# Staging table rows in the attention's buffers, and 13 gather buffers instead of 10

## The chip, the core and the metric

The kernel runs on one core of a Trainium2 chip. A core has five engines, each with an instruction queue of its own: TensorE (PE in the profile; PEld is its weight load), VectorE (DVE), ScalarE (ACT), GpSimd (POOL) and SyncE (SP), which only issues transfers here. Sixteen DMA engines move data between HBM, the large memory, and SBUF, the memory on the core; matmuls write to PSUM, which DVE and ACT read. Engines wait for one another by semaphores. The metric is the time of one execution in microseconds (us), from the device.

## The reference

Two layers act on a tensor `x` of 8 images, 256 channels and 64 x 64 points; all is in float32. Each is a group norm (32 groups of 8 channels), a layer, and a residual. The first layer is an attention over each point's 3 x 3 neighbours in 4 heads, to which weights that a small projection generates are added. The second is a deformable convolution: for each output point and each of 9 taps it reads the image at a computed, fractional position.

```python
x = x + _L0_conv_ref(_gn(x), w_qkv, w_kg, b_kg, alpha, beta, w_proj)
x = x + _L1_conv_ref(_gn(x), w_off, b_off, w)
...
# layer 0
qkv = einsum('oc,bchw->bohw', w_qkv, x)
q, k_, v = split(qkv, 3, axis=1)
logits = einsum('bhdl,bhdkl->bhkl', q, patches3x3(k_))
attn_out = einsum('bhkl,bhdkl->bhdl', softmax(logits, axis=2), patches3x3(v))
kernel = einsum('hkc,bhcl->bhkl', w_kg, qkv_by_head) + b_kg
conv_out = einsum('bhkl,bhdkl->bhdl', kernel, patches3x3(v))
out = einsum('oc,bchw->bohw', w_proj, alpha * conv_out + beta * attn_out)
...
# layer 1
om = conv3x3(x, w_off) + b_off                  # 27 channels
off, mask = om[:, :18], sigmoid(om[:, 18:27])   # (dy, dx) of 9 taps; a mask of each
py, px = base_y + ky + off_y, base_x + kx + off_x
y0, x0 = floor(py), floor(px); ly, lx = py - y0, px - x0
v = (samp(y0, x0) * (1 - ly) * (1 - lx) + samp(y0, x0 + 1) * (1 - ly) * lx
     + samp(y0 + 1, x0) * ly * (1 - lx) + samp(y0 + 1, x0 + 1) * ly * lx) * mask
out = einsum('bckhw,ock->bohw', v, w)
```

`samp(y, x)` takes all channels of one point, and zeros outside the image.

## The kernel before, in words

**Two halves run beside each other.** For each image there is a *front*: the attention (`attention`, line 595) and then the preparation of the convolution (`prepare`, line 678). And there is the deformable convolution itself, in the main loop (line 977). While image `b` is convolved, the front of image `b + 1` is issued in small steps between the pieces of the convolution. The generator `fronts` yields after each step. `STEPS` = 144 steps belong to the stretch of one image, about one for each half slot of the main loop (lines 998 to 1002). The front of the first image runs alone at the start, and during the last image there is none.

The order of instructions on PE, ACT, DVE and POOL is the order in which the program calls them (`manual_schedule`, line 949); each engine executes its queue in order. SyncE issues its transfers in order too.

**Table and gathers.** An image is cut into 8 chunks of 8 rows (512 points). In `prepare`, each chunk passes `to_table` (line 684), then `offsets` (18 matmuls, line 710), and one step later `positions` (line 722). `to_table` writes the normalized chunk, transposed to one row per point, to a table in HBM. An entry holds a point's 256 channels and those of the point one image row below; since two entries follow one another, one row of 4 KB fetches all four corners. In three parts per chunk, PE transposes 176 points into PSUM (`ptab`, line 690), ACT copies them to an SBUF tile `ts` (line 696), and SyncE issues two writes of 176 KB from it (line 699), one for each half of the entries. Two tables take turns between images. `positions` turns the offsets into an index and four corner weights for each point and tap.

The convolution of an image is 72 slots (8 chunks x 9 taps) of 4 blocks of 128 points, so 288 blocks. For a block, POOL issues a gather (`gather`, line 838) that fetches one 4 KB row for each of 128 points into a buffer `g`; ACT scales the first corner into a tile `s` (`scale`, line 854); DVE adds the other three in three instructions (`sum_corners`, line 862), after which `g` is free; PE transposes `s` into PSUM (`pt`, line 892); ACT copies that to `vt` (line 895); and four matmuls of a slot's 512 points add to the output `po` (line 917). At the end of a chunk ACT copies `po` to `y` (line 932), DVE adds the residual, and SyncE stores the result (line 939); `r`, the residual, is loaded again from a copy in HBM at line 904.

**How far ahead.** When the main loop stands at block `i`, ACT scales blocks `i` + 8 and `i` + 9 (`SCALE_AHEAD`), DVE sums `i` + 6 and `i` + 7 (`SUM_AHEAD`), and POOL issues the gathers of `i` + `LEAD` and the next, where `LEAD` = `SCALE_AHEAD` + `GATHERS` = 18. There are `GATHERS` = 10 buffers `g` of 4 KB per partition (pool `gp`, line 104). In the last image, `gathers` also has POOL write a mark (`tick`) every fourth block, which DVE copies one slot later (line 872). After some long pieces of the attention POOL copies one element of their result (`held`, line 881), which holds its next gathers until DVE or ACT is done.

**Buffers.** A tag with `bufs=n` names `n` buffers that are used in turn. A tile that takes a buffer over waits until all that read the tile before it, transfers included, are done. The buffers that matter here, per partition: `ts`, six of 2 KB (line 695); `qk`, one of 6.25 KB, with the attention's products of queries and keys (line 373; `logits` reads it); `wk`, four of 2 KB, with the spread attention weights (line 523; `weighted` reads it). An attention's last use of `qk` and `wk` lies before `prepare` begins.

**Other loads.** While the table is written, SyncE also loads the next image in chunks of 512 KB (`load_chunk`, line 93), each after its place in `image` has been normalized for the table. DVE takes their statistics (`first_stats`, line 289), and after the last one `Norm` forms mean and variance (`mv`, line 185); the first matmul of the next attention (`gn`, line 190) needs them.

Of the kernel before, what the change touches and what calls it, by code (L numbers as in the profile page):

```python
# [9 lines left out]
F32 = mybir.dt.float32  # L10
# [8 lines left out]
C = 256  # L19
# [9 lines left out]
HEADS = 4  # L29
# [5 lines left out]
TJ = 6  # L35
TP = R * WP // TJ
# [11 lines left out]
BLOCKS = SLOTS * NB  # L48
SUM_AHEAD = 6
SCALE_AHEAD = SUM_AHEAD + 2  # L50
GATHERS = 10
LEAD = SCALE_AHEAD + GATHERS
STEPS = 2 * SLOTS
STEPS_AHEAD = 12
# [5 lines left out]
def preact_kernel(ctx: ExitStack, tc: tile.TileContext, a: dict, out: bass.AP):  # L60
# [30 lines left out]
    def load_chunk(b, c, queue=nc.sync):  # L91
        s = slice(c * N, (c + 1) * N)
        queue.dma_start(image[:, :, s], sources[b][:, :, s])
# [8 lines left out]
    for c in (0, 2, 4, 6, 7):  # L102
        load_chunk(0, c)
    gp = ctx.enter_context(tc.tile_pool(name="gp", bufs=GATHERS))
    w_qkv = [gp.tile([96, 4, C], F32, tag="g", name=f"w_qkv{i}") for i in range(2)]
# [61 lines left out]
    p1 = ctx.enter_context(tc.tile_pool(name="p1", bufs=1))  # L167
    p2 = ctx.enter_context(tc.tile_pool(name="p2", bufs=2))
# [6 lines left out]
    def psum_a(name):  # L175
        return ps_a.tile([P, 512], F32, tag="a", name=name)
# [501 lines left out]
    def prepare(b, gn):  # L678
# [5 lines left out]
        def to_table(c, xn):  # L684
            for i in range(TJ // 2):
                ps = psum_a(f"ptab_{b}_{c}_{i}").rearrange("p (j e) -> p j e", j=2)
                for j in range(2):
                    o = WP + (2 * i + j) * TP
                    for ct in range(NT):
                        nc.tensor.transpose(  # L690
                            ps[:TP, j, ct * P : (ct + 1) * P],
                            xn[:, ct].rearrange("p r w -> p (r w)")[:, o : o + TP],
                            ident,
                        )
                ts = p2.tile([TP, 2, C], F32, tag="ts", name=f"ts_{b}_{c}_{i}", bufs=6)
                nc.scalar.copy(ts, ps[:TP])
                for q in range(2):
                    e = (R * c + 1 - q) * WP + 2 * i * TP
                    nc.sync.dma_start(
                        table[e : e + 2 * TP, q, :].rearrange("(j p) e -> p j e", p=TP), ts  # L700
                    )
# [92 lines left out]
        for c in range(NC):  # L794
            if om is not None:
                positions(c - 1, om)
            to_table(c, xn)
            yield
            om = offsets(c, xn)
            if b + 1 < B and c > 0:  # L800
                first_stats(b + 1, c - 1)
            if c + 1 < NC:
                xn = normed(xt, gn, c + 1, carry=True)
            if b + 1 < B:
                if c == 0:
                    load_chunk(b + 1, 0)
                if c + 1 < NC:
                    load_chunk(b + 1, c + 1)
            yield
# [22 lines left out]
    def gather(i):  # L832
        if i >= B * BLOCKS:
            return
        b, n = divmod(i, BLOCKS)
        c, k, j = n // NB // KK, n // NB % KK, n % NB
        g = gp.tile([P, 4 * C], F32, tag="g", name=f"g_{i}")
        nc.gpsimd.indirect_dma_start(  # L838
            out=g,
            out_offset=None,  # L840
            in_=tables[b % 2],
            in_offset=bass.IndirectOffsetOnAxis(ap=found[b, c][0][:, j, k : k + 1], axis=1),
        )
        rows[i] = g
# [12 lines left out]
    def sum_corners(i):  # L857

        work = [sums[n] for n in (i, i + 1) if n in sums]
        for q in range(1, 4):  # L860
            for s, g, w in work:
                nc.vector.scalar_tensor_tensor(  # L862
                    s, g[:, q * C : (q + 1) * C], w[:, q : q + 1], s, ALU.mult, ALU.add
                )
# [84 lines left out]
    with tc.manual_schedule(engines=ordered):  # L949
# [8 lines left out]
        for n in range(STEPS_FIRST - 4):  # L958
            next(steps, None)
        for i in range(GATHERS):  # L960
            gather(i)
        for i in range(0, SUM_AHEAD, 2):
# [5 lines left out]
            sum_corners(i)  # L968
            gather(i + GATHERS)
            gather(i + GATHERS + 1)  # L970
            for n in range(2 if i == 0 else 1):
                next(steps, None)
        done = STEPS + STEPS_FIRST
        gather(SUM_AHEAD + GATHERS)
        gather(SUM_AHEAD + GATHERS + 1)
# [105 lines left out]
```

## Time and profile before

| | |
|---|---|
| median of 4 runs | 4811.95 us (4808.81 to 4822.01) |
| profiled execution | 4811.06 us, span 4809.3 us |
| mean granted TensorE clock | 0.988 |
| start, until the first block is transposed | 338 us |
| images 1 to 7, each | 566 to 581 us |
| last image | 443 us |
| DVE line 862, sums | 6912 of 475 ns |
| POOL line 838, gathers | 2304 of 1264 ns |
| PE line 917, convolution | 4608 of 601 ns |
| ACT line 696, copies to `ts` | 192 of 588 ns or less |

The span runs from the first instruction to the last. "PE pt L892 <- DVE s L862" in a view of waits reads: PE stood idle before the instruction of line 892 that writes `pt`, and what released it was DVE's instruction that writes `s`. In a timeline, a row gives start, duration, engine, line, operation, names (out<-in) and a count of merged instructions; the bracket holds the idle time before it and what ended it. In a view of windows, a row gives a stretch, its length, each engine's busy time with its count of instructions, the granted clock, the mean busy share of the DMA engines and their GB/s.

### The profile page before, as it was taken

The numbers are of one execution on the slowest core, as the hardware profiler recorded it, in microseconds if no ns is written. First come the engines' busy times: TensorE is split into PE (matmuls) and PEld (weight loads), VectorE is DVE, ScalarE is ACT, GpSimd is POOL, SyncE is SP. The second block draws the span as 40 slices with busy tenths as digits, with TensorE's granted clock in tenths as the row PEclk, the third lists the DMA queues.
The fourth block names the chain that finished last, engine by engine and source line by source line (L and its number), as shares of the span: only waits on it lengthen the run. The fifth ranks groups of instructions, "written<-read, shape, count | busy, mean of one in ns | idle before, by whom it ended". The sixth has DMA issues, their size and how long they took to land. (4 is left out here: it accounts for less than half of the span.)

```text
span 4809.3 us, 77468 instructions
## 1 busy us (share of the span) xinstructions
PE 4555.1 (95%) x25344; PEld 2362.5 (49%) x25344; DVE 4178.0 (87%) x10177; ACT 2442.1 (51%) x5200; POOL 3005.4 (62%) x2607
## 2 busy tenths in 40 slices
PE   8989999999999999999999999999999899997878
PEld 4444554455544555445544555545554455543434
DVE  5669889899988998899998999889998899987887
ACT  2335555455555555555554555555555455554554
POOL 0027666676656666477675766757666676667786
PEclk9999999999999999999999999999999999999999
DMA  2068789888898888988889888888888888888998
GB/s 98 23 219 289 275 295 335 296 315 297 299 338 302 306 287 286 361 291 306 298 300 346 298 301 286 326 324 285 305 304 326 289 304 288 291 317 333 358 354 311
DMA packets 472353, 1414.03 MB, mean 294 GB/s; under 512 B 46526, under 2 KB 114366, under 8 KB 471820
## 3 DMA queue, kind: packets, MB, share of 16 engines
q0 software_dynamic: 331776, 1208.11, 70.1%
q1 hardware_dynamic: 138156, 197.62, 11.6%
q8 instruction: 199, 3.26, 0.3%
q10 hardware_dynamic: 2016, 3.36, 0.2%
q14 instruction: 206, 1.69, 0.1%
HBM read 1275.97 MB, written 132.94 MB: 293 GB/s over the span
## 5 line engine op out<-in xcount | busy, mean ns | idle before, releaser
L838 POOL DMA_INDIRECT g<-table,idx x2304 | 2911.6, 1264 | 1779.6 <-DVE s L862 622.6
L862 DVE SCALAR_TENSOR_TENSOR s<-g,wt,s 128x256 f32<-128x256 f32 x6912 | 2809.1, 475 | 110.3 <-ACT s L854 98.3
L917 PE MATMUL po<-vt,w_conv 128*128 128x512 f32 x4608 | 2191.2, 601 | 2.1 <-ACT y L932 2.1
L854 ACT ACTIVATE s<-g,wt 128x256 f32<-128x256 f32 x2304 | 1077.6, 509 | 377.0 <-DMA g<-table,idx 297.0
L917 PEld LDWEIGHTS po<-vt,w_conv 128*128 128x128 f32 x4608 | 819.6, 192 | 830.0 <-issue 817.7
L895 ACT COPY vt<-pt 128x512 f32<-128x512 f32 x1152 | 617.2, 588 | 608.2 <-PE pt L892 607.8
L892 PE MATMUL pt<-ident,s 128*128 128x128 f32 x4608 | 654.4, 279 | 121.0 <-DVE s L862 108.5
L892 PEld LDWEIGHTS pt<-ident,s 128*128 128x128 f32 x4608 | 520.7, 141 | 355.9 <-DVE s L862 146.4
L391 DVE TENSOR_TENSOR qk<-qk,near_k 128x400 f32<-128x400 f32 x256 | 134.8, 568 | 238.5 <-PE qk L383 238.5
L710 PE MATMUL om<-xn,w_off 128*32 128x512 f32 x2304 | 288.8, 598 | 0.0
L309 PE MATMUL psq<-xn,w_qkvT 128*128 128x512 f32 x512 | 254.3, 641 | 26.4 <-DVE wk L524 22.9
L340 PE MATMUL psv<-xn,w_qkvT 128*128 128x512 f32 (+1 forms) x576 | 249.8, 560 | 2.1 <-DVE kb L442 2.1
L340 PE MATMUL psk<-xn,w_qkvT 128*128 128x512 f32 (+1 forms) x576 | 246.3, 557 | 0.0
L570 PE MATMUL proj<-acc,w_projT 128*128 128x512 f32 x512 | 239.6, 593 | 1.6 <-ACT acc L564 1.6
L317 ACT COPY q<-psq 128x512 f32<-128x512 f32 x128 | 75.1, 586 | 248.9 <-PE psq L309 248.9
L309 PEld LDWEIGHTS psq<-xn,w_qkvT 128*128 128x128 f32 x512 | 97.5, 200 | 179.3 <-issue 89.3
L351 ACT COPY k<-psk 128x512 f32<-128x512 f32 (+1 forms) x144 | 79.2, 551 | 192.2 <-PE psk L340 192.2
L557 PEld LDWEIGHTS av<-wk,vk 100*64 100x64 f32 x4096 | 130.9, 138 | 92.3 <-issue 34.1
L710 PEld LDWEIGHTS om<-xn,w_off 128*32 128x32 f32 x2304 | 74.3, 109 | 200.5 <-issue 161.7
L544 ACT COPY vk<-vk 100x512 f32<-100x512 f32 x256 | 137.4, 587 | 69.7 <-PE vk L539 69.4
L340 PEld LDWEIGHTS psk<-xn,w_qkvT 128*128 128x128 f32 x576 | 104.1, 190 | 123.1 <-issue 118.7
L340 PEld LDWEIGHTS psv<-xn,w_qkvT 128*128 128x128 f32 x576 | 103.3, 190 | 118.0 <-issue 114.6
(102 smaller groups left out, 3439.9 us busy)
## 6 DMA issues: line engine op xcount, KB each, us to landing
table<-ts SPq DMA_DIRECT2D x384, 176.0 KB
g<-table,idx POOLq DMA_INDIRECT x2304
x<-in_x_dram SPq DMA_DIRECT2D x61, 512.0 KB
x<-x SPq DMA_DIRECT2D x56, 512.0 KB
r<-x SPq DMA_DIRECT2D x56, 512.0 KB
out_dram<-r SPq DMA_DIRECT2D x56, 512.0 KB
out_dram<-y SPq DMA_DIRECT2D x7, 512.0 KB
w_conv<-in_w_conv_dram SPq DMA_DIRECT2D x1, 2304.0 KB
```

The costliest lines, as they stand in the source:

```text
L309: nc.tensor.matmul(ps, w_qkvT[:, ct, m * P : (m + 1) * P], window(self.xn, ct, 4), start=(ct == 0), stop=(ct == NT - 1),)
L340: nc.tensor.matmul(ps[:, : (hi - lo) * W], w_qkvT[:, ct, o : o + P], self.xn[:, ct, lo:hi, 1 : W + 1], start=(ct == 0), stop=(ct == NT - 1),)
L391: nc.vector.tensor_mul(qk[:, 2 * jj : 2 * jj + 2, :, h, :], both[h][:, : 4 * NK].rearrange("p (j c k) -> p j c k", j=2, c=NT), near_k.unsq ...
L544: nc.scalar.copy(self.vk[:, 2 * j : 2 * j + 2, :].rearrange("p t c -> p (t c)"), ps[:NK])
L570: nc.tensor.matmul(ps, w_projT[:, ct, m * P : (m + 1) * P], self.acc[:, ct].rearrange("p (t y x) -> p y t x", y=T, x=T), start=(ct == 0), ...
L710: nc.tensor.matmul(ps[32 * g : 32 * g + 32, :], w_off[:, ct, k, :], window(xn, ct, k), start=(n < 4), stop=(n >= KK * NT - 4),)
L838: nc.gpsimd.indirect_dma_start(out=g, out_offset=None, in_=tables[b % 2], in_offset=bass.IndirectOffsetOnAxis(ap=found[b, c][0][:, j, k : ...
L854: nc.scalar.activation(s, g[:, 0:C], AF.Copy, scale=w[:, 0:1])
L862: nc.vector.scalar_tensor_tensor(s, g[:, q * C : (q + 1) * C], w[:, q : q + 1], s, ALU.mult, ALU.add)
L892: nc.tensor.transpose(pt[ct][:, j, :], s[:, ct * P : (ct + 1) * P], ident)
L895: nc.scalar.copy(v[:, ct, :], pt[ct].rearrange("p b n -> p (b n)"))
L917: nc.tensor.matmul(po[m], w_conv[:, ct, k, m * P : (m + 1) * P], v[:, ct, :], start=(k == 0 and ct == 0), stop=(b + 1 < B and k == KK - 1 ...
```

## The change

Three more gather buffers are kept, 13 for 10, so `LEAD` becomes 21. The room comes from `ts`, whose six buffers of 2 KB go. For an odd chunk, the three parts are tiles of the tag `wk`, one of its four buffers after another. For an even chunk, one tile of the tag `qk` holds all three parts; ACT copies to a third of it at a time.

```diff
-GATHERS = 10
+GATHERS = 13
 LEAD = SCALE_AHEAD + GATHERS
...
-                ts = p2.tile([TP, 2, C], F32, tag="ts", name=f"ts_{b}_{c}_{i}", bufs=6)
+                if c % 2:
+                    ts = p2.tile([TP, 2, C], F32, tag="wk", name=f"ts_{b}_{c}_{i}", bufs=HEADS)
+                else:
+                    if i == 0:
+                        whole = p1.tile(
+                            [TP, TJ // 2, 2, C], F32, tag="qk", name=f"ts_{b}_{c}"
+                        )
+                    ts = whole[:, i]
                 nc.scalar.copy(ts, ps[:TP])
                 for q in range(2):
                     e = (R * c + 1 - q) * WP + 2 * i * TP
```

## The prediction

> **What bounds the kernel now.** I read the page's engine row first, then the waits of TensorE (PE) over the whole span, then windows, then the timelines of the places where PE waits.
>
> ```profile
> PE 4555.1 (95%) x25344; PEld 2362.5 (49%) x25344; DVE 4178.0 (87%) x10177; ACT 2442.1 (51%) x5200; POOL 3005.4 (62%) x2607
> q0 software_dynamic: 331776, 1208.11, 70.1%
> q1 hardware_dynamic: 138156, 197.62, 11.6%
> ```
> PE is the bound for most of the time, so a change of buffers can only win what PE waits: 4809.3 - 4555.1 = 254 us, and of that only what late gathers cause. The gathers (q0) hold the DMA engines for 70% of the span and SyncE's transfers (q1: table rows, images, outputs) for 12%.
>
> ```profile
> PE pt L892 <- DVE s L862: 108.5, 89, 6.8
> PE gn L190 <- DVE mv L185: 45.1, 9, 9.1
> PE pt L892 <- ACT vt L895: 11.9, 15, 2.6
> ACT s L854 <- DMA g<-table,idx: 297.0, 305, 7.3
> ACT ts L696 <- DMA table<-ts: 31.7, 17, 3.3
> ```
> The first row sounds like the target. By time, though, 80.0 us of it lie in the last image and 11.0 in the seventh. "Image n" here is the time in which the nth image is convolved; from the end of the seventh no next image's work runs beside it. Each of images 1 to 6 has 2 to 5 us. ACT (ScalarE) waits 297 us for gathers, but it is busy for 51%, and most of that reaches nobody.
>
> The windows show where gathers are late: the light stretch at the end of an attention (lines 658 to 676), where little front work slows the convolution.
>
> ```profile
> 1338.00:1376.00 38.00, 32.58 (x149) 16.06 (x148) 30.86 (x80) 18.46 (x36) 29.34 (x27) 1.00 0.97 368
> 1376.00:1456.00 80.00, 75.92 (x471) 35.52 (x469) 73.26 (x213) 39.20 (x87) 31.18 (x32) 1.00 0.98 363
> 1913.00:1951.00 38.00, 33.28 (x145) 16.51 (x144) 30.15 (x77) 18.95 (x37) 29.17 (x25) 0.96 0.98 365
> ```
> The columns are PE, weight loads, DVE (VectorE), ACT and POOL (GpSimd) busy, granted clock, DMA share and GB/s. PE is idle for about 5 of 38 us. From there until the next image's attention begins (second row: the stage that writes the table) DMA is at 0.98. How it starts, on DVE and POOL:
>
> ```profile
> 1325.30 11.95 DVE L862 SCALAR_TENSOR_TENSOR s<-g,wt,s 128x256 f32<-128x256 f32 x30
> 1328.09 9.97 POOL L838 DMA_INDIRECT g<-table,idx  x1 [2.58 <-DVE s L862]
> 1338.37 0.93 POOL L838 DMA_INDIRECT g<-table,idx  x1 [0.30 <-issue]
> 1343.64 0.51 ACT L854 ACTIVATE s<-g,wt 128x256 f32<-128x256 f32 x1 [1.86 <-DMA g<-table,idx]
> 1349.32 0.33 PE L892 MATMUL pt<-ident,s 128*128 128x128 f32 x1 [2.60 <-ACT vt L895]
> 1357.11 0.84 PE L892 MATMUL pt<-ident,s 128*128 128x128 f32 x4 [1.03 <-DVE s L862]
> ```
> DVE runs 30 sums back to back; for that time POOL hangs in one gather (9.97 us instead of 0.93). The ten buffers are used up, ACT waits for the next gather, its copies of `vt` come late behind that wait, and PE stops.
>
> **The change, part by part.** *Removed, added.* No instruction: 192 copies of 588 ns on ACT and 384 table writes on SyncE stay; only their buffers differ. Cost 0 for both.
>
> *The copies' waits.* Before, six `ts` buffers: each copy waits for the copy two chunks earlier to have landed. After, an even chunk fills one buffer of three parts in the place of `qk`, so its first copy waits for all six writes of the chunk two before; an odd chunk rotates through four `wk` buffers, so its first copy waits for nothing recent and the other two for one copy further back. With the landings of the trace's completion records (image 2: chunk 0 done at 1385.2, chunk 2 at 1411.1, chunk 4 at 1430.0; the copies begin at 1385.7, 1410.1, 1430.8), even chunks wait about 1 us more at chunk 4 and odd ones 2 to 3 us less at chunk 3: over all images about 23 us for today's 31.7. Neither counts: ACT waits 2.77 and 1.30 us in chunk 3 of image 2 and PE has no gap over 0.53 us in that stage until its end. The cover is the 18 offset matmuls (10.8 us a chunk) queued on PE. If it is gone, ACT's wait goes through `s` to DVE, which is 92% busy there; that price is in the slower rival.
>
> *`qk` and `wk` at both ends.* The first chunk's copy needs the last attention chunk's readers, done tens of us before; the next image's first `qk` write comes 30 us after chunk 6 has landed (1450.6 in image 2), its first `wk` write later still. Cost 0.
>
> *The first gather of the next image* is issued three gathers earlier, and needs the whole table. Table landed and the issue it now takes: 889.1 and 892.6, 1463.6 and 1467.9, 2038.8 and 2044.7, 2619.2 and 2619.5, 3190.3 and 3195.2, 3766.0 and 3773.9. At most 3 us of POOL waiting with 21 blocks in hand: cost 0. Every gather moves up by three in POOL's queue; the tick and hold copies stay where they are.
>
> *Three more gathers landed when POOL hangs.* POOL issues one per 0.94 + 0.30 = 1.24 us when free, so they are worth 3.7 us of lateness at each light stretch. PE's gaps there (over 0.25 us, on `pt`) are 2.1, 4.2, 2.6, 2.8, 2.6, 2.3 and 2.6 us: 19.2. A gap of 0.6 at the end of each stands without a late gather, so 7 x 0.6 = 4.2 stay: 15.0 go. The stretches of images 3 to 6 also show a clock of 0.96 (third window for image 3), 4 x 0.04 x 38 = 6.0 us. Gain 21.0: 2.0 in image 7, 19.0 in the first six (3.2 each).
>
> *What is late next.* After the stage, PE waits for `gn`: mean and variance need the last chunk of the next image.
>
> ```profile
> 1432.07 8.35 SPq L699 DMA_DIRECT2D table<-ts  x6
> 1440.51 1.82 SPq L939 DMA_DIRECT2D out_dram<-r  x1
> 1442.42 0.62 SPq L93 DMA_DIRECT2D x<-in_x_dram  x1
> 1454.40 1.29 DVE L289 BATCH_NORM_STATS2 stats<-x 128x6 f32<-128x512 f32 x2 [0.50 <-DMA x<-in_x_dram]
> 1456.24 0.38 PE L190 MATMUL gn<-mv,gmat 128*128 128x2 f32 x2 [3.71 <-DVE mv L185]
> ```
> That load stands in SyncE's queue behind the table writes. The six gaps are 5.3, 3.7, 6.4, 3.1, 5.6, 9.1 us, and DVE's wait for the load before them 2.1, 0.5, 3.2, 0, 2.4, 6.3: the gap is 3.1 plus that wait. So a microsecond won earlier is kept only if this load also lands earlier. The granted clock after the gaps (0.66 over 10 us after 5.3, 0.83 after 3.7, 0.61 over 13 us after 9.1) costs 18.7 us for 33.2 us of gap: 0.56 us more per us.
>
> The writes start with PE and so 3.2 us earlier, but refilling 13 buffers takes longer. POOL issues 27 gathers in the 38 us before the stage (0.71 per us, its few small copies counted in) and 32 in its 80 (0.40), so three more take 3 / 0.31 = 9.7 us. During the refill SyncE's six writes take 11.0 and 11.7 us, 0.53 per us, against a need of about 8 transfers per 10.4 us chunk (six writes, an image load, a store or reload: 0.77): 2.3 transfers, or 3.0 us, fall behind. In image 2 SyncE's lag behind the copies drains (8.3 us at chunk 3, 1.3 at chunk 6); in images 3 and 6 it does not (3.6, 5.3 at chunk 6). Ends: 0 and 3.0. I take 1.3, a little under the middle, as four of six drain. The gap grows by 1.3 x 1.56 = 2.0 us in six images: 12.0 back.
>
> The Trainium skill ("DMA: Bandwidth & Descriptors", Queues, rings and completion order) states that each DMA engine takes turns between the queues that have work, whatever their length. By it the table writes keep their share however deep the gathers queue; the trace agrees that they get through, at 0.53 per us. The rule alone would not lengthen a single write, and the sum would be 12.0 us better.
>
> *The last image.* POOL and DVE pace each other there by the tick copies (DVE waits 73.8 us for POOL's marks); the gather issued at block `i` reuses the buffer of block `i` + LEAD - GATHERS = `i` + 8, before and after, so the pace of 1.5 us a gather stays. What changes is the stock at its start. Upper end 3 x 1.5 = 4.5 us. Lower end 0: DVE's run of 30 sums at 4332.75 would go on over the three landed blocks, and POOL, hanging from 4335.55 for 9.98 us, would hang longer by as much. I take the middle, 2.2.
>
> The Trainium skill ("SBUF — State Buffer", SBUF: two separate sides) speaks against the change here: DVE can hold a port pair that GpSimd needs for its descriptors, and the loser blocks for whole instructions. By it a deeper stock only lengthens the block, and this term would be 0.
>
> *Sum.* 19.0 + 2.0 - 12.0 + 2.2 = 11.2 us. The profiled execution took 4811.06 us (span 4809.3), the median of the runs is 4811.95; less 11.2 that is 4799.9 to 4800.8, and I say **4800**.
>
> **The rivals.** *Hidden anyway*: DVE's longer runs lengthen POOL's hangs in every light stretch, or the load for `gn` gives all back. For it: the gap at `gn` follows that load. Against it: at 1337.25 DVE's run ends at the projection, not for want of blocks. Image 7's 2.0 stays: 4809.
>
> *All kept*: the lag drains in every image, 19.0 + 2.0 + 4.5 = 25.5: 4786. For it: image 4, with no wait on the load. Against it: images 3 and 6.
>
> *Slower*: the load for `gn` lands later in absolute time. If six images lose their 3.2 and the full 3.0 us of lag comes on top, the gap grows by 6.2, PE's loss is 6.2 x 1.56 - 3.2 = 6.5 each, 39 in all, less 2 to 4 in the last two images: 4847. It decides from where the load is later by 2.1 us than the copies before it (2.1 x 1.56 = 3.2); past 0.2% from 3.5 us of lag. ACT's waits at even chunks push the same way, since they delay DVE before `mv`.
>
> **How the numbers follow.** About 0.2% (9.6 us) is what a measurement of this kernel can tell from no change. Forecast (part kept) 0.38; all kept 0.15; hidden 0.22; slower 0.25. The forecast's own range, by a lag of 0.6 to 2.0 us and 0 to 4.5 in the last image, is 4791 to 4809, two thirds of it faster by over 0.2%. Faster: 0.15 + 0.27 + a little of the hidden case, 0.45; same 0.28; slower 0.27. The range reaches the all-kept end and into half of the slower case: 4784 to 4828.
>
> **What would show it.** Right: ACT's waits for gathers fall well below 297 us, PE's waits on `pt` in the light stretches nearly vanish, the gaps at `gn` grow by about 1 us each, the last image keeps about 443 us. ACT's waits for table writes move from odd chunks to even ones and stay near 30 us. Wrong if the gaps at `gn` stay (then faster than 4790) or reach 10 us and more with the clock near 0.6 after them, if DVE's runs and POOL's hangs grow past 12 us, or if the last image changes its pace.

## The result: no difference that can be measured

| | before | after |
|---|---|---|
| median of runs taken side by side on one chip | 4810.69 us (63 runs, 4803.19 to 4825.9) | 4814.53 us (42 runs, 4797.96 to 4820.49) |
| ratio of the times, with its 95% interval | | 1.0002 [0.9996, 1.0007] |
| profiled execution, and its span | 4811.06, 4809.3 us | 4800.93, 4799.1 us |

By the ratio the change moves the time by -0.04% to +0.07%: nothing. (The means of the listed runs, 4811.42 and 4812.33 us, have this ratio; the medians alone lie 0.08% apart.) The gain of 11 us that was forecast is not there. One warning on reading the profile of after: its execution is among the shortest of its runs, 14 us under their median, so its sums explain 4801 us and not the median. They show where time moves inside the program; the ratio says what it comes to.

**The profile after.** The page's rows that answer to those of before, and two of its groups by line:

```profile
PE 4550.4 (95%) x25344; PEld 2364.9 (49%) x25344; DVE 4178.6 (87%) x10177; ACT 2411.4 (50%) x5200; POOL 3022.7 (63%) x2607
q0 software_dynamic: 331776, 1208.11, 70.2%
q1 hardware_dynamic: 138156, 197.62, 11.6%
...
L845 POOL DMA_INDIRECT g<-table,idx x2304 | 2921.3, 1268 | 1748.1 <-DVE s L869 593.8
L861 ACT ACTIVATE s<-g,wt 128x256 f32<-128x256 f32 x2304 | 1047.2, 508 | 105.2 <-DMA g<-table,idx 89.7
```

The work is the same to the instruction and the packet. The lines of the convolution have moved by 7 (`gather` is L845, `scale` L861, `sum_corners` L869, `pt` L899; the `ts` copy is L703, its writes L706). Next the waits over the whole span:

```profile
PE pt L899 <- DVE s L869: 103.4, 82, 5.4
ACT s L861 <- DMA g<-table,idx: 89.7, 73, 9.1
DVE stats L289 <- DMA x<-in_x_dram: 55.1, 17, 7.1
PE gn L190 <- DVE mv L185: 44.3, 9, 9.3
ACT ts L703 <- DMA table<-ts: 30.4, 12, 8.1
PE ptab L690 <- DVE xn L259: 18.5, 10, 4.5
```

ACT's wait for gathers fell from 297.0 to 89.7 us: the deeper stock does what it should. Two waits of this list grew: DVE's for the image chunks that SyncE loads (39.8 before), and PE's for `xn` before the table's transposes (8.8 before). The second follows from the first: DVE stands at the statistics of a chunk, and the normalization of the next chunk stands behind them in DVE's queue. In image 5, from the timeline:

```profile
3116.41 6.32 SPq L706 DMA_DIRECT2D table<-ts  x2
3122.83 2.35 SPq L93 DMA_DIRECT2D x<-in_x_dram  x1
3123.06 1.29 DVE L289 BATCH_NORM_STATS2 stats<-x 128x6 f32<-128x512 f32 x2 [5.45 <-DMA x<-in_x_dram]
3125.20 1.77 PE L690 MATMUL ptab<-ident,xn 128*88 128x128 f32 x12 [2.85 <-DVE xn L259]
...
3178.54 1.28 DVE L289 BATCH_NORM_STATS2 stats<-x 128x6 f32<-128x512 f32 x2 [6.14 <-DMA x<-in_x_dram]
...
3180.39 0.59 PE L190 MATMUL gn<-mv,gmat 128*128 128x2 f32 x2 [9.35 <-DVE mv L185]
```

Before, such waits cost PE time almost only at the last chunk, at `gn`. Now they do so in the middle of the stage as well; the sums follow.

**Where the time moved.** I cut the time of each image by three events on PE: the last spread of weights of an attention, the first transpose for the table, and the matmul `gn`. From the first to the second is the *light stretch*, from the second to the third the *stage* in which the table is written; all else until the next light stretch is the rest. The light stretch of image n lies in the time in which image n is convolved; the stage of image 7 is counted to the first transpose of the last image. This light stretch begins earlier than the windows of the prediction (in image 2 of before it runs from 1320.9 to 1361.9 us, there the window from 1338 to 1376), so it holds POOL's hang: that is why its DMA share is 0.75 below and 0.97 there. Sums from the trace, in us:

| | before | after | |
|---|---|---|---|
| start, until the light stretch of image 1 | 749.6 | 747.2 | -2.4 |
| light, images 1 to 6 | 240.9 | 220.9 | -20.0 |
| stage, images 1 to 6 | 575.1 | 594.6 | +19.4 |
| rest, images 1 to 6 | 2636.6 | 2629.4 | -7.2 |
| image 7, light and stage | 40.4 + 123.6 | 37.0 + 125.3 | -1.7 |
| last image | 443.0 | 444.7 | +1.7 |

What the light stretches won, the stages gave back, nearly to the microsecond. Of the 19.4 us, some 14 are idle time of PE (39.5 to 53.6): the waits at `ptab` went from 2.7 to 17.3 and those at `gn` from 33.3 to 32.5. About 5.4 are lost clock (4.8 to 10.2: the sum over the records of a reduced clock of length times the missing share).

The windows of image 4 show both halves. The columns are PE, weight loads, DVE, ACT and POOL busy, granted clock, DMA share, GB/s; in each fence the light stretch stands first and the stage second. Before:

```profile
2473.00:2513.00 40.00, 37.12 (x192) 20.15 (x188) 32.99 (x82) 20.89 (x42) 29.56 (x23) 0.96 0.75 278
2513.00:2608.00 95.00, 89.43 (x557) 42.91 (x557) 87.19 (x251) 47.09 (x102) 44.20 (x38) 1.00 0.98 365
```

After:

```profile
2468.00:2505.00 37.00, 35.38 (x193) 19.45 (x189) 33.89 (x84) 21.11 (x43) 28.11 (x20) 1.00 0.72 267
2505.00:2603.00 98.00, 90.58 (x556) 44.14 (x555) 86.39 (x247) 46.56 (x100) 47.88 (x41) 0.98 0.97 365
```

DMA has a quarter of the light stretch free in both, and almost nothing free in the stage. Share times length, both rows added, is the *DMA work* between the two ends: 123.1 us before and 121.7 after. Averaged over images 2 to 6 it is 124.9 and 124.2. The light stretch is shorter, the DMA engines have the same work to do before `gn`, and so the stage is longer. The gathers' packets show it: over images 2 to 6, the light stretch moves 18.8 gathers (of 128 packets of 4 KB) before and 15.8 after, the stage 41.2 and 44.0. By the first transpose for the table both kernels have the same number behind them, 238; the three more are made up in the stage, which is 3.4 us longer for 3.3 us more of DMA work. The work is not quite a fixed bill, since part of it may come after `gn`: of the 8448 packets of 1 KB that write a table, some 930 (before) and 1000 (after) do. This reading became theory D below.

### The profile page after: what moved, and what is told of

Same layout as the page of the kernel before. It is cut to its first block, busy times and chain, and to the rows that moved or that the text cites. A ratio compares the mean times of both kernels' runs of the same rounds, so it can differ in the third digit from the quotient of the medians.

```text
span 4799.1 us, 77506 instructions
## 1 busy us (share of the span) xinstructions
PE 4550.4 (95%) x25344; PEld 2364.9 (49%) x25344; DVE 4178.6 (87%) x10177; ACT 2411.4 (50%) x5200; POOL 3022.7 (63%) x2607
## 3 DMA queue, kind: packets, MB, share of 16 engines
q1 hardware_dynamic: 138156, 197.62, 11.6%
## 5 line engine op out<-in xcount | busy, mean ns | idle before, releaser
L845 POOL DMA_INDIRECT g<-table,idx x2304 | 2921.3, 1268 | 1748.1 <-DVE s L869 593.8
L869 DVE SCALAR_TENSOR_TENSOR s<-g,wt,s 128x256 f32<-128x256 f32 x6912 | 2805.9, 475 | 63.1 <-ACT s L861 62.7
L861 ACT ACTIVATE s<-g,wt 128x256 f32<-128x256 f32 x2304 | 1047.2, 508 | 105.2 <-DMA g<-table,idx 89.7
L899 PE MATMUL pt<-ident,s 128*128 128x128 f32 x4608 | 653.5, 279 | 110.0 <-DVE s L869 103.4
L899 PEld LDWEIGHTS pt<-ident,s 128*128 128x128 f32 x4608 | 521.7, 142 | 342.2 <-DVE s L869 148.8
L309 PE MATMUL psq<-xn,w_qkvT 128*128 128x512 f32 x512 | 252.6, 638 | 25.8 <-DVE wk L524 21.4
L557 PEld LDWEIGHTS av<-wk,vk 100*64 100x64 f32 x4096 | 131.4, 139 | 92.3 <-issue 34.1
L340 PEld LDWEIGHTS psv<-xn,w_qkvT 128*128 128x128 f32 x576 | 103.0, 190 | 117.4 <-issue 114.1
```

Of the source, the lines that this page charges most:

```text
L309: nc.tensor.matmul(ps, w_qkvT[:, ct, m * P : (m + 1) * P], window(self.xn, ct, 4), start=(ct == 0), stop=(ct == NT - 1),)
L340: nc.tensor.matmul(ps[:, : (hi - lo) * W], w_qkvT[:, ct, o : o + P], self.xn[:, ct, lo:hi, 1 : W + 1], start=(ct == 0), stop=(ct == NT - 1),)
L845: nc.gpsimd.indirect_dma_start(out=g, out_offset=None, in_=tables[b % 2], in_offset=bass.IndirectOffsetOnAxis(ap=found[b, c][0][:, j, k : ...
L861: nc.scalar.activation(s, g[:, 0:C], AF.Copy, scale=w[:, 0:1])
L869: nc.vector.scalar_tensor_tensor(s, g[:, q * C : (q + 1) * C], w[:, q : q + 1], s, ALU.mult, ALU.add)
L899: nc.tensor.transpose(pt[ct][:, j, :], s[:, ct * P : (ct + 1) * P], ident)
```

## The experiments

Each kernel was compared with the kernel before on the same chip. The chips differ: the kernel before took 4887.78 us in the first set, 4874.53 in the second, 5077.32 in the third and 4839.6 in the last, so only ratios are compared across sets. On these chips the kernel before was timed but not profiled; a length beside one of another set may differ by the chip. The letters of the expectations: **L** is the prediction's own mechanism, image loads that land late behind the refill; **W** its rival, that the copies to `ts` lose time in the buffers they were moved to; **D**, formed after the first set, that the DMA work of light stretch and stage together is the limit; **E**, the rival to D, that PE and DVE themselves bound the stage. The averages over images 2 to 6, in us:

| kernel | ratio [95%] | light | stage | both | DMA work |
|---|---|---|---|---|---|
| before | | 41.0 | 95.8 | 136.9 | 124.9 |
| after | 1.0002 [0.9996, 1.0007] | 37.1 | 99.2 | 136.3 | 124.2 |
| `ts_only` | 1.0001 [0.9992, 1.001] | 41.0 | 97.0 | 138.1 | 125.1 |
| `more_stages` | 0.9983 [0.9974, 0.9992] | 37.2 | 101.4 | 138.6 | 124.9 |
| `x_act_13` | 1.0011 [1.0001, 1.0021] | 37.1 | 103.3 | 140.4 | 125.6 |
| `x_act_10` | 0.9998 [0.9989, 1.0007] | 40.8 | 98.1 | 138.9 | 124.9 |
| `half_10` | 0.9959 [0.9947, 0.9972] | 41.0 | 92.0 | 133.0 | 118.8 |
| `half_13` | 0.9895 [0.9881, 0.991] | 37.0 | 92.1 | 129.1 | 116.6 |
| `tick_10` | 0.9977 [0.9967, 0.9987] | 37.9 | 95.6 | 133.5 | 125.8 |
| `tick_13` | 0.9954 [0.9941, 0.9968] | 37.9 | 95.2 | 133.0 | 125.7 |
| `after_again` | 1.0016 [1.0004, 1.0028] | 38.1 | 103.0 | 141.1 | 128.3 |
| `cap_13` | 0.9966 [0.9952, 0.998] | 37.7 | 98.5 | 136.3 | 124.0 |
| `tick_13_stages` | 1.0005 [0.9994, 1.0016] | 39.2 | 102.2 | 141.4 | 131.4 |
| `tick_cap_13` | 0.9917 [0.9891, 0.9943] | 37.9 | 94.3 | 132.2 | 125.6 |

**The new buffers alone** (`ts_only`): the copies go to `qk` and `wk`, with ten gather buffers.

```diff
-GATHERS = 13
+GATHERS = 10
```

> The table rows in qk and wk, but 10 gather buffers as before. Two theories of where the change's gain went. L: refilling 13 gather buffers delays SyncE's transfers, and PE waits for the image loads among them. W: an even chunk's copies wait for all writes of the chunk two before, ACT stands, and DVE and PE lose it. L expects the time of before, 4811 +- 3 us, with the light stretch at the end of an attention as long as before (41 us). W expects the stage that writes the table to be longer by 2 to 3 us in each of seven images, so 4825 to 4832 us.

4889.3 us for 4887.78: nothing. Light and stage are those of before to about 1 us, and ACT's wait for table writes is 26.8 us where it was 31.7. The new place of `ts` costs nothing by itself with ten buffers, as L expected; W alone explains none of the give-back.

**More places for the copies, with 13 buffers** (`more_stages`): even chunks alternate between `qk` and two buffers of the attention's tags `q` and `vk`.

```diff
-                    if i == 0:
-                        whole = p1.tile([TP, TJ // 2, 2, C], F32, tag="qk", ...)
-                    ts = whole[:, i]
+                    if c % 4 == 0:
+                        if i == 0:
+                            whole = p1.tile([TP, TJ // 2, 2, C], F32, tag="qk", ...)
+                        ts = whole[:, i]
+                    else:
+                        if i == 0:
+                            whole = p1.tile([TP, 2, 2, C], F32, tag="q", ...)
+                        if i == 2:
+                            whole = p1.tile([TP, 2, 2, C], F32, tag="vk", ...)
+                        ts = whole[:, i % 2]
```

> 13 gather buffers; even chunks take turns between qk and the buffers of q and vk, so that a copy waits for the chunk four before. ACT's waits for table writes (33 us in all after the change) should fall to near 0 by either theory. W expects the light stretches' 20 us to be kept then: about 4792 us. L expects the time of the change, 4814 +- 4 us, with DVE still waiting for the image loads, 5 to 10 us per image.

0.9983, faster by 8 us: small, but with an interval below 1, and neither theory's number (L had no gain, W 20 us). The copies' waits for table writes fell to 13.3 us, not to near 0, and the stage is no shorter for it: 101.4 us. With the copies free to run ahead, the loads are later still:

```profile
DVE stats L289 <- DMA x<-in_x_dram: 60.6, 16, 9.6
PE gn L190 <- DVE mv L185: 38.2, 9, 8.6
PE ptab L690 <- DVE xn L259: 28.5, 13, 8.1
```

So W falls for the stage, though its waits are there: taking them away moves the loss to `ptab`. Beside `ts_only` on the same chip, the seven light stretches are 21.5 us shorter and the stages of images 1 to 6 21.4 us longer; the 11.8 us between the two profiles lie in the rest of the images (9.0) and at the start (3.7), for which neither theory has a reason.

**The image loads on another queue** (`x_act_13` and, with ten buffers, `x_act_10`): ACT issues the loads, so that they no longer stand behind the table writes on SyncE.

```diff
-                    load_chunk(b + 1, c + 1)
+                    load_chunk(b + 1, c + 1, nc.scalar)
```

> The changed kernel with the next image's loads issued by ACT, not by SyncE, so that they do not stand behind the table writes. L expects DVE's waits for the loads (7 to 12 us per image) and PE's gaps before gn (32 us in six images) to fall by more than half and the light stretches to stay at 37 us: 4785 to 4795 us. W expects no change of time, 4814 us, and ACT still waiting 33 us for table writes with PE's gaps moving to other places.

> The kernel before with the same move of the loads to ACT, 10 gather buffers. L expects a gain at the gaps before gn alone, with light stretches still at 41 us: 4795 to 4803 us, and x_act_13 faster than it by 10 to 20 us. If the loads are not what holds PE, 4811 us, and no difference between the two.

The loads are on time now, and the stage of `x_act_13` is longer, not shorter. Its waits:

```profile
ACT s L861 <- DMA table<-ts: 67.2, 7, 15.4
PE omt L733 <- ACT om L726: 42.4, 18, 9.3
PE gn L190 <- DVE mv L185: 27.7, 9, 5.1
DVE stats L289 <- DMA x<-in_x_dram: 10.3, 7, 3.7
```

DVE's waits for loads fell from 55.1 to 10.3 us and the sum of the six gaps at `gn` from 32.5 to 16.0 (14.8 with ten buffers). In their place ACT stands for up to 15.4 us where it issues a load while table writes are outstanding, and PE waits behind it at the offsets (`omt`). The ratios are 1.0011 and 0.9998. L had expected 16 to 26 us less than before for `x_act_13`; W's "no change" was nearer. So L's wait is real, but moving the loads out of SyncE's queue does not shorten the stage: whoever issues a transfer waits there. Whether ACT's wait is for the DMA engines or for something in how two queues share a completion the trace does not say.

**Half of the table writes left out** (`half_10`, `half_13`), from the third image's table on, so those images are computed from incomplete tables. This takes work from DMA and nothing from PE.

```diff
-                for q in range(2):
+                for q in range(1 if b > 1 else 2):
```

> The kernel before, 10 gather buffers, with half of the table writes left out from the third image on (each entry keeps an old second half, so the output is not the reference's). The theory after the first four runs, D: light stretch and table stage together are set by the DMA work that must pass in them, so what a deeper stock wins in the one it gives back in the other. D expects the light stretch to stay at 41 us and the table stage to shorten from 96 to 93 or 94 us (gaps before gn near their floor of 2.5 to 3 us): 15 to 25 us less than before. The rival, E: the stage is bound by PE and DVE themselves, and gaps only move about; then within 8 us of before.

> The changed kernel with the same half of the table writes left out from the third image on. D expects the light stretch at 37 us and the stage at 93 to 95 us, so that the gain of the 13 buffers is kept: 15 to 25 us less than half_10. E expects no difference from half_10 beyond 5 us.

`half_10` is 21.5 us below before, as D expected and E did not. With less DMA work in the stage, the stages of the two kernels are equal (92.0 and 92.1 us, a little below D's 93 to 95), and the light stretch stays short with 13 buffers: the gain is kept. 4820.44 us against 4853.08, 32.6 us less on the same chip, more than D's 15 to 25, where the whole change is worth nothing with all writes. The windows of image 4, `half_10`:

```profile
2466.00:2507.00 41.00, 37.96 (x197) 20.36 (x196) 34.00 (x85) 20.89 (x42) 30.70 (x23) 0.96 0.76 279
2507.00:2599.00 92.00, 88.76 (x556) 42.84 (x556) 87.07 (x250) 46.89 (x102) 44.33 (x38) 1.00 0.96 349
```

and `half_13`:

```profile
2453.00:2490.00 37.00, 35.38 (x196) 19.40 (x189) 33.87 (x85) 20.78 (x43) 28.23 (x20) 1.00 0.73 264
2490.00:2582.00 92.00, 88.90 (x557) 42.73 (x556) 86.74 (x248) 46.61 (x101) 48.25 (x42) 1.00 0.98 366
```

With ten buffers DMA has a little room left (0.96); with 13 the same 92 us hold the refill as well (0.98), and PE does not feel it. Of the 34.9 us between the two spans, 22.4 are the seven light stretches, 4.4 the rest, 4.4 the start, 3.5 the last image. The left-out packets (4224 per image of 1 KB, 46 ns each in the trace, over 16 engines: 12.1 us) are more than the fall of the DMA work, 6.1 and 7.6 us. The packets' records say why: the 1 KB packets between the two events fall by 9.5 and 9.3 us only, since with all writes the last of them came after `gn`, and the gathers' packets there take more time, 178 for 172 ns on average in `half_10` and 174 for 171 in `half_13`, which is up to 3.2 us. And the edit takes work from the engines and transfers from SyncE's queue at once, so it does not tell these two apart; `cap_13` below does.

**Using the idle DMA of the light stretch** (`tick_10`, `tick_13`): POOL's marks, which in the last image make DVE pause between runs of sums, are also set at blocks 208 and 212 of every image and in the last 24 blocks of image 7.

```diff
-        if i >= (B - 1) * BLOCKS and i % NB == 0:
+        late = i >= (B - 1) * BLOCKS - 24 or 208 <= i % BLOCKS < 216
+        if late and i % NB == 0:
```

> The kernel before, with the tick copies of the last image also at two places of each image's long run of sums (blocks 208 and 212) and over the last 24 blocks of the seventh image, so that DVE pauses and POOL's gather is not held for 10 us. D expects the hang to fall to 1 to 3 us, DMA to work on in that time, and light stretch and table stage together to shorten by 3 to 8 us per image: 20 to 50 us less than before. The rival, E: DVE loses about 5 us per image in the pauses and has none to spare; 0 to 30 us more than before.

> The changed kernel with the same ticks. D expects 20 to 50 us less than before, and about the same as tick_10, since with DMA busy the stock of 3 more gathers is worth little. E expects 0 to 30 us more than the changed kernel.

D says that using the 25% of free DMA before the stage must pay, with ten buffers too. It does: 0.9977 and 0.9954, and E's "more" falls. The size was missed: `tick_10` gains 11.6 us where D had 20 to 50, while `tick_13` is in that range with 23.9. The hang is cut into pieces, and POOL issues between them. The timeline of `tick_13` in image 5, first DVE:

```profile
3035.62 4.83 DVE L869 SCALAR_TENSOR_TENSOR s<-g,wt,s 128x256 f32<-128x256 f32 x12
3042.65 0.15 DVE L879 COPY marks<-marks 128x1 f32<-128x1 f32 x1 [2.20 <-POOL marks L886]
3042.76 4.86 DVE L869 SCALAR_TENSOR_TENSOR s<-g,wt,s 128x256 f32<-128x256 f32 x12
3048.58 0.15 DVE L879 COPY marks<-marks 128x1 f32<-128x1 f32 x1 [0.96 <-POOL marks L886]
```

then POOL:

```profile
3038.42 2.85 POOL L845 DMA_INDIRECT g<-table,idx  x1 [2.58 <-DVE s L869]
3041.57 0.94 POOL L845 DMA_INDIRECT g<-table,idx  x1 [0.30 <-issue]
```

The hang is 2.85 us, and another behind it 3.98, where it was one of 9.97 in after. The light stretch of image 4 has a DMA share of 0.87 for 0.72:

```profile
2460.00:2498.00 38.00, 35.62 (x196) 19.50 (x193) 34.74 (x89) 21.59 (x45) 26.16 (x24) 1.00 0.87 299
2498.00:2594.00 96.00, 90.12 (x560) 43.10 (x559) 86.75 (x249) 45.16 (x98) 46.70 (x40) 1.00 0.98 366
```

DMA work is unchanged (125.7), both stretches together are 3.3 us an image shorter than in after (whose profile is from another chip). Beside each other, 13 buffers are worth 12.3 us here (4862.95 to 4850.64); D had expected about nothing.

**Not refilling in the stage** (`cap_13`, beside `after_again`, which is after unchanged). The 13 buffers stay, but while the main loop stands at blocks 228 to 261 of an image, gathers are issued four blocks later, which holds the stock at about ten. By the trace of image 4 it is filled up from 9 us before `gn` on, so some of the refill lands behind `gn`, in the next attention.

```diff
-        gather(i + LEAD)
-        gather(i + LEAD + 1)
+        upto = i + LEAD + 2
+        if i < (B - 1) * BLOCKS and 228 <= i % BLOCKS < 262:
+            upto -= 4
+            if state["next"] < upto:
+                nc.gpsimd.tensor_copy(held, sums[i + SUM_AHEAD + 1][0][:, 0:1])
+        while state["next"] < upto:
+            gather(state["next"])
+            state["next"] += 1
```

> The changed kernel itself on the same chip as the two runs below, for a second profile of it and as their measure. D expects the same work of the DMA engines (124 to 126 us per image between the last spread of weights and the matmul of gn, as in the kernel before and in six of the runs) and a ratio to before of 1.000 +- 0.001.

> The changed kernel, with the stock held at 10 gathers while the table is written (blocks 228 to 261 of each of the first seven images; POOL copies one element of the newest sum before it gathers on) and filled up to 13 afterwards, in the attention, where DMA has room. D expects light stretches of 37 us as with 13 buffers, 3 x 1.3 = 3.8 us less DMA work in the stage, and the stage 2 to 4 us shorter: 10 to 25 us less than the changed kernel. E, by which the stage is bound by PE and DVE, expects 0 to 10 us more, for the added copies.

On this chip after is 0.16% slower than before, with 128.3 us of DMA work: both outside what D had expected of it. `cap_13` is 23.4 us faster than after (5063.33 for 5086.68), as D expected and E did not. The light stretch keeps its length, the stage is 4.5 us an image shorter, and the DMA work in the two together falls by 4.3. SyncE's transfers are the same and in the same order, only gathers come later: both kernels have issued the same ones when `gn` starts, but 41.4 gathers instead of 42.7 move within the stage, most of the held ones at its end. So it counts when gathers load the engines, and not the order of SyncE's queue alone. The waits, though, stand elsewhere than in the first profile of after. `after_again`:

```profile
ACT om L726 <- remote: 62.3, 6, 13.5
PE omt L733 <- ACT om L726: 48.0, 16, 9.6
PE gn L190 <- DVE mv L185: 27.0, 9, 5.2
DVE stats L289 <- DMA x<-in_x_dram: 7.7, 5, 3.7
```

`cap_13`:

```profile
ACT om L726 <- remote: 36.8, 4, 10.8
PE omt L733 <- ACT om L726: 25.8, 12, 6.9
PE gn L190 <- DVE mv L185: 20.7, 6, 5.1
DVE stats L289 <- DMA x<-in_x_dram: 12.2, 6, 4.5
```

Here the loads were nearly on time in both, and ACT stood before its copy `om` for up to 13.5 us until something came that the profile doesn't name ("remote"), and PE behind it at the offsets. The cap cut that by 40%. So which wait carries the loss changes from chip to chip. What ACT waited for here stays open, and with it whether DMA work alone makes the stage that long: the longest stages of all (102 to 103 us, `after_again`, `x_act_13` and `tick_13_stages`) have DMA shares of 0.95 to 0.97, below the 0.98 of before and after. With part of the refill put off, the 13 buffers are a gain here.

**Together.** `tick_13_stages` has the marks and `more_stages`; `tick_cap_13` the marks and the cap.

> The changed kernel with the ticks in the long runs of sums and with the table rows in three sets of buffers, so that copies hardly wait. If the gains of the two changes (0.2% and 0.5% in their own runs) add up, 0.993 of before; if both fill the same DMA time, 0.995 to 0.996, no better than the ticks alone.

> The changed kernel with both remedies: ticks in the long runs of sums, so that DMA does not stand during POOL's hang, and the stock held at 10 while the table is written. By D they act at two places (DMA idle before the stage, DMA work in it) and add up: light stretch and stage together 4 to 8 us per image shorter than in the changed kernel, 0.991 to 0.995 of before. If one uses up what the other frees, 0.995 to 0.997, as each alone.

`tick_13_stages` missed: 1.0005, with a stage of 102.2 us, on the chip with the slowest stages. Two gains of other chips did not add up there, and neither part ran on that chip alone, so which of them failed is open. `tick_cap_13` beats the kernel before, 4803.48 us for 4839.6, **0.9917 [0.9891, 0.9943]**, and by this ratio after as well, which was not run on this chip. The windows of its image 4:

```profile
2456.00:2493.00 37.00, 34.62 (x191) 19.32 (x188) 33.74 (x86) 21.56 (x45) 25.40 (x23) 1.00 0.86 300
2493.00:2588.00 95.00, 89.21 (x560) 43.16 (x558) 87.40 (x250) 45.23 (x98) 51.10 (x55) 0.98 0.98 368
```

A short light stretch with DMA in use, and a stage no longer than before. Both together are 4.1 us an image shorter than in after's profile, at the lower end of what was expected.

## Where the prediction was right, and where it was wrong

The time, 4814.53 us, lies within the outer range of 4784 to 4828, but above the forecast's own 4791 to 4809: the gain of 11.2 us did not come. That the profiled execution took 4800.93 us, next to the 4800 forecast, is luck: the stage and the last image came out 7.4 and 3.9 us worse than forecast, and 9.6 us at the start and in the rest of the images, which were not forecast, made up for most of it.

- **The gain in the light stretch: right.** Forecast 21.0 us, of it 15.0 in waits and 6.0 in clock; in the profile 23.4 in seven images, with PE's idle time there down by 14.0 (21.2 + 4.1 to 9.8 + 1.5) and the clock at 1.00. In every pair of kernels with 10 and 13 buffers and without marks the stretch went from about 41 to 37 us.
- **The give-back: the step that failed.** It was "The gap grows by 1.3 x 1.56 = 2.0 us in six images: 12.0 back". The profile shows 19.4 us, 3.2 an image. Divided by the same 1.56 that is a lag of 2.1 us, inside the ends that were given (0 and 3.0) and just the point from which nothing is left of the gain. I took 1.3 because in four of six images SyncE's lag drained in the profile of before; that reasoned from a stage that still had ten buffers to fill. What was missing is the balance that the runs show: the DMA engines of the stage are busy for 0.97 to 0.98, as the prediction's own windows say, so the three gathers that the shorter stretch no longer moves (18.8 to 15.8) are paid for in full behind it (41.2 to 44.0).
- **Its place was wrong too.** The load behind the table writes was the right wait, but not only the last load: the gaps at `gn` did not grow (33.3 to 32.5), and the loss stands at `ptab` (2.7 to 17.3) and in the clock. The sign by which I meant to judge, gaps at `gn` that stay, was named as a sign of a time under 4790; it was not.
- **The rule on queues.** The Trainium skill ("DMA: Bandwidth & Descriptors", Queues, rings and completion order) has engines take turns between queues, by which the sum would have been 12.0 us better. The runs differ from that reading: with equal DMA work the loads came later, 39.8 to 55.1 us of waiting, and `cap_13` won 4.5 us a stage by only issuing gathers later. Turns between the queues made no room in engines that were busy for 0.98 of the time.
- **Copies and new buffers, cost 0: right but for one wait.** `ts_only` is 1.0001. The waits moved to even chunks, all but some 2 us of them, and are 30.4 us where the sum had about 23; one of them reached PE: the 8.1 us at chunk 4 of image 7, after which PE waited 2.7 us at `omt`.
- **First gather of the next image, cost 0: right.** POOL's wait for the table is 0.3 us in all.
- **The last image: the lower end, 0, and not 2.2.** DVE's run of sums went from 30 to 37 and POOL's hang with it, as these rows of after show; before, they were 30 sums and 9.98 us:

```profile
4321.64 14.73 DVE L869 SCALAR_TENSOR_TENSOR s<-g,wt,s 128x256 f32<-128x256 f32 x37
...
4324.44 12.73 POOL L845 DMA_INDIRECT g<-table,idx  x1 [3.94 <-DVE s L869]
```

The last image took 444.7 us for 443.0. Here the Trainium skill ("SBUF — State Buffer", SBUF: two separate sides) states that DVE and GpSimd share a pair of ports, which one of them can hold for a whole instruction while the other blocks. The trace agrees in that POOL's gather ended only 0.8 us behind DVE's run, after 12.73 us; that the ports are the reason, and over a run of 37 instructions, no run here shows.

- **The rivals.** What happened is *hidden anyway* by its second clause, "the load for `gn` gives all back", at other chunks than its last. Its first clause did not happen: in the light stretches the hang is 9.97 us before and after. *All kept* fails by the stage; of *slower* (4847 us, 0.7% more) the most that was seen is 1.0016, on the third chip.
- **Not forecast, not explained:** the rest of the images got shorter by 7.2 us in six. It did so in the other pairs with 10 and 13 buffers too (`ts_only` to `more_stages` 9.0, `x_act_10` to `x_act_13` 5.2, `half_10` to `half_13` 4.4, `tick_10` to `tick_13` 5.6); I tested no cause. The profile's terms sum to -10.2 us, and the medians show none of it. The runs of after reach over 23 us, and the longer ones have the lower mean granted clock (0.988 in the three with the highest, 4799 us on average; 0.983 in the three with the lowest, 4820 us). With one profile of it on that chip I can't say which waits these lose their clock to.

## What to carry to other kernels

These rules come from one kernel. Before you count a wait that a deeper buffer removes, look at the share of the resource that refills it in the stretch that follows: where it is full, the refill is paid there, and the sum of both stretches is what moves. Take the share of the DMA engines times the length from one fixed event to the next; if a change leaves that product as it is and no idle share is used, expect no gain. Then the time to win is where the resource idles (here a quarter of the light stretch, while POOL hung) and in moving refills to where it has room.

## What the runs showed of the hardware

- The DMA work between two fixed points of the program was 124.0 to 125.8 us in ten of the fourteen profiles, and moved only where transfers were left out (118.8, 116.6) or on the third chip (128.3 and 131.4; 124.0 with the cap, which puts gathers off).
- POOL's hang in one gather follows the run of DVE's sums: 9.97 us with 30 sums, 12.73 with 37, 2.85 and 3.98 where DVE paused after 12.
- Chips differ in single stages and not evenly. The last image took 443 to 445 us on the first chip, 500 to 516 on those of the first two sets of experiments, 438 to 450 on the third set's and 468.6 on the last; the rest of images 1 to 6 took 2626 to 2637 us on all but the third set's, where it took 2836 to 2852. A kernel compared with another on a second chip would have shown 0.6 to 5.5% that no edit made.
